# Attention scores in PSUM by halves of the queries: three single banks for scores, four for other products, aims set anew

## The chip, the cores and the metric

The kernel runs on one core of one Trainium2 chip. The metric is the device time of one execution in microseconds (us); lower is better. In the profile, PE is TensorE's matmuls and PEld its weight loads, DVE is VectorE, ACT is ScalarE, POOL is GpSimd and SP is SyncE.

## What is computed

Two graph layers are applied to 16 elements of a batch. An element has 1024 nodes with 256 features (`x`) and an integer adjacency matrix of 1024 by 1024 (`adj`).

The first layer is attention with 8 heads of 32 features, with a leaky slope in place of a scale, and a mask:

```python
q, k, v = heads(features @ Wq), heads(features @ Wk), heads(features @ Wv)
e = einsum('whqd,whkd->whqk', q, k)
e = where(e >= 0, e, 0.2 * e)
attn = softmax(where(adj > 0, e, -9e15), axis=-1)
h = concat_heads(attn @ v)
out = concat([layernorm(h), features]) @ Wffn.T
x1 = layernorm(out) + features
```

The second layer is a graph attention done twice, then a feed-forward block with 1024 hidden values:

```python
Wh = h @ W
e = leaky_relu(Wh @ a[:F] + (Wh @ a[F:]).T, 0.2)
h = softmax(where(adj > 0, e, -9e15), axis=1) @ Wh      # twice: (W1, a1), (W2, a2)
h = layernorm(x1 + h)
out = layernorm(h + relu(h @ w_ff1 + b_ff1) @ w_ff2 + b_ff2)
```

All values are fp32. The kernel uses exponentials without subtracting a maximum (`unshifted_path`); a flag, worked out at its end, would start a general path if the sums or scores left safe limits. In these runs it doesn't.

## The kernel before: stages, order and names

Work is cut into tiles of 128 nodes, 8 tiles (`NT`) an element. The 16 elements `b` are overlapped in a software pipeline: while the scores of element `b` are made, the rest of element `b - 1` (its layer norms, the two graph attentions, the feed-forward block of the element before) and the projections of element `b + 1` (transposes of x, q, k, v, the mask) are fitted between them.

The order of every engine's instructions is written out ahead by a planner, the class `Order`. Each piece of work is a Python generator that yields steps: `on(PE=450)` says that the next instructions occupy an engine for so many ns by the planner's own estimate, `take` and `give` handle a place in a pool of buffers, `wait` and `fire` handle events between pieces. Where several pieces could start within 300 ns (`WINDOW`), the one with the smallest due time (its aim) is put first. An aim is a share of a slot (`SLOT`, 253 us) after the start of the element's scores, from the table `AIM` (`EARLY` for the first two elements). The chip then runs each engine's queue strictly in that order, and each instruction waits for its operands and its buffer; no time of the planner is kept on the chip.

The pieces that matter here:

- `load_stacks` (L536 and on) loads `qs` and `ks`, the operands of one head's scores, by SP's queue (L554). `all_scores` (L567) multiplies them (L587): for a tile `t` of keys it makes a tile `ps_s` of 128 keys by 1024 queries, in two matmuls of 512 columns, one for each PSUM bank. Element 0 takes one such tile at a time, the others two at once, so four matmuls stand in a row. The pool `scores` has two tiles of two banks each.
- `weights` (L594) scales a tile by 0.2 from PSUM into `p` in SBUF (ACT, L605; in element 0 also DVE, L603), takes the maximum of that and the scores on DVE (L607), which frees the tile's two banks, takes the exponential on ACT (L610) and multiplies by the mask on POOL (L614). There are five `p` buffers.
- `all_values` (L617) multiplies `p` of two tiles by v into the one bank `ps_a` (L636; output rows of the two query halves are placed at partitions 0 and 64).
- Every other product goes to the pool `misc`, three single banks `ps_m`: transposes (L355, L417, L663, L807, L915), q and k (L470), v (L499), rows (L739, L742, L771), the two graph products `second_rows` (L862) and `normed_pair` (L887), and the feed-forward block (L927, L955). A bank is freed when ACT or DVE has copied it out (L311 and L313, L475, L506 and L508, L670, L774, L870, L933 and L936 among others).
- `attend` (L824, L827, L830, L832) makes a tile of graph attention on DVE and scales rows on ACT, eight tiles a layer, two layers an element.
- `mask_part`, `x_pair` and `qk_part` issue the loads of `adj` and `x` (ACT's queue) and the stores of q and k halves (SP's queue).

So PSUM's eight banks are: scores 2 x 2, misc 3, values 1. `lead` in `AIM` bounds how far ahead of its due time a score may be put, `fast0`, `fast1` and `fast15` scale the pace of the scores in the first two and the last element.

Of the kernel before, what the change touches and what calls it, by code (L numbers as in the profile page):

```python
# [9 lines left out]
FT = mybir.dt.float32  # L10
# [4 lines left out]
AF = mybir.ActivationFunctionType  # L15
OP = mybir.AluOpType

ALPHA = 0.2
EPS = 1e-5
H = 8  # L20
P = 128
HALF = 512
# [155 lines left out]
def on(shared=False, delay=0.0, **costs):  # L178
    return "on", (costs, shared, delay)
# [6 lines left out]
def wait(event):  # L186
    return "wait", event


def fire(event):  # L190
    return "fire", event


def take(pool):
    return "take", pool


def give(pool):
    return "give", pool


def start(thread, aim):
    return "start", (thread, aim)
# [21 lines left out]
def unshifted_path(  # L225
# [8 lines left out]
    nc = tc.nc  # L234
    B, N, D = x.shape
    NT = N // P
# [5 lines left out]
    NH = N // HALF  # L242
# [4 lines left out]
    YW = D + 2  # L247
    NSUM = NT * H + 2 * NT
    NSCORE = 4 * NT
    SLOT = 253e3  # L250
    PACE = SLOT / (H * NT // 2)


    AIM = dict(mask0=0.759, x=0.818, x_step=0, mask=0.747, mask_step=0.0264, qk0=0.614, qk1=0.898,
               qk_step=0.0231, v0=0.832, v1=0.974, v_step=0.0591, rows=-0.244, rows_step=0.0408, first0=0.12,
               first1=0.252, graph0=-0.009, graph1=0.21, graph_step=0, second=0.355, second_step=0.0335,
               normed=0.78, normed_step=0.026, ff_wait=(None, 0, 1, 0), ff=(0.532, -0.011, 0.487, 0.497),
               ff_step=0.0386, fast0=0.425, fast1=0.938, fast15=0.832, lead=3.15)

    EARLY = dict(x=0.87, x_step=0.005, mask=0.747, mask_step=0.0296, qk0=0.692, qk1=0.909, qk_step=0.0345,  # L260
                 v0=0.774, v1=1.001, v_step=0.0568, rows=-0.139, rows_step=0.0071, first0=0.082, first1=-0.169,
                 graph0=-0.195, graph1=-0.027, graph_step=0, second=0.302, second_step=0.0335, normed=0.781,
                 normed_step=0.02, ff_wait=(None, 0, 1, 0), ff=(0.633, -0.001, 0.488, 0.497), ff_step=0.0386)
# [3 lines left out]
    small = ctx.enter_context(tc.tile_pool(name="small", bufs=6))  # L267
    psum = ctx.enter_context(tc.tile_pool(name="psum", bufs=2, space=bass.MemoryType.PSUM))
    dram = ctx.enter_context(tc.tile_pool(name="dram", bufs=3, space=bass.MemoryType.DRAM))
    bufs = dict(misc=3, scores=2, acc=1, p=5, stacks=2, stage=2, adj=2, adjb=2, pair=18,  # L270
                xT=2, v=2, mask=2, hn=1, w8=2, big=1, job=1)
    work = Order(**bufs)

# [111 lines left out]
    stacks = {}  # L385
# [41 lines left out]
    def make_mask(b, t0):  # L427
# [3 lines left out]
        for n, (t, halves) in enumerate(parts):  # L431
            yield start(mask_part(b, t, halves),
                        t0 + ((share(b - 1, "mask") if b else AIM["mask0"]) + share(b - 1, "mask_step") * n) * SLOT)

# [123 lines left out]
    probs = {}  # L558
# [8 lines left out]
    def all_scores():  # L567
        for b in range(B):
            yield wait(("stack", b, 0))
            t0 = begin[b] = work.now  # L570
            if b + 1 < B:
                yield start(project(b + 1, t0), t0)
            for h in range(H):
                yield wait(("stack", b, h))
                q, kk = stacks[b, h]
                n = 2 if b else 1
                for t in range(0, NT, n):
                    due = t0 + (h * NT + t) / 2 * pace(b)
                    yield aim(due, AIM["lead"] * PACE)
                    for _ in range(n):  # L580
                        yield take("scores")
                    ps = [psum.tile([P, N], FT, tag="scores", name="ps_s") for _ in range(n)]
                    yield on(PE=450 * n)
                    for i in range(n):
                        for nh in range(NH):
                            cols = slice(nh * HALF, (nh + 1) * HALF)
                            nc.tensor.matmul(ps[i][:, cols], kk[:, (t + i) * P:(t + i + 1) * P], q[:, cols],  # L587
                                             start=True, stop=True)
                    if t + n == NT:
                        yield give("stacks")  # L590
                    for i in range(n):
                        yield start(weights(b, h, t + i, ps[i]), due + i * PACE / 2)

    def weights(b, h, t, ps):  # L594
        yield take("p")
        p = buf([P, N], "p", "p")
        probs[b, h, t] = p
        if b == 0:
            engine = yield on(ACT=1050, DVE=1230)
        else:  # L600
            engine = yield on(ACT=1050)
        if engine == "DVE":
            nc.vector.tensor_scalar(p, ps, ALPHA, None, op0=OP.mult)  # L603
        else:
            nc.scalar.activation(p, ps, AF.Copy, scale=ALPHA)  # L605
        yield on(DVE=1220)
        nc.vector.tensor_tensor(p, p, ps, op=OP.max)  # L607
        yield give("scores")
        yield on(ACT=1080)
        nc.scalar.activation(p, p, AF.Exp)  # L610
        for tt in range(NT):
            yield wait(("mask", b, tt, t // TPH))
        yield on(POOL=2050, shared=True)
        nc.gpsimd.tensor_tensor(p, p, mask_of(b, t), op=OP.mult)  # L614
        yield fire(("p", b, h, t))
# [815 lines left out]
```

## Time and profile before

| | |
|---|---|
| median of 3 runs | 4489.06 us (4487.12 to 4491.18) |
| profiled execution | 4494.55 us, span 4492.7 us |
| mean granted TensorE clock | 0.99 |
| busy: PE, DVE, ACT, POOL | 4326.9, 3315.8, 2886.4, 2472.5 us |
| scores: ACT L605, DVE L607, 128x1024 | mean 1025 and 1214 ns, 993 and 1024 times |
| exponential L610, mask product L614 | mean 1058 and 2195 ns, 1024 times each |
| score matmul L587, start to start in a row | about 233 ns, 2048 times |

The page of a profile gives busy time by engine, then the span in 40 slices (tenths busy), then the queues of DMAs, a chain of work followed back from the end, and groups of instructions by line. The other views used here answer from the same trace: busy time in stretches of the span that one chooses, waits (an engine's idle time, put down to the instruction that ended it), and a timeline of single instructions, in which neighbours of one kind are merged (x2, x8). An fp32 matmul of the program stands twice in the trace, that of the scores once. A busy PE is not PE at its peak, since matmuls overlap.

### The profile page before, as it was taken

The numbers are of one execution on the slowest core, as the hardware profiler recorded it, in microseconds if no ns is written. First come the engines' busy times: TensorE is split into PE (matmuls) and PEld (weight loads), VectorE is DVE, ScalarE is ACT, GpSimd is POOL, SyncE is SP. The second block draws the span as 40 slices with busy tenths as digits, with TensorE's granted clock in tenths as the row PEclk, the third lists the DMA queues.
The fourth block names the chain that finished last, engine by engine and source line by source line (L and its number), as shares of the span: only waits on it lengthen the run. The fifth ranks groups of instructions, "written<-read, shape, count | busy, mean of one in ns | idle before, by whom it ended". The sixth has DMA issues, their size and how long they took to land.

```text
span 4492.7 us, 57101 instructions
## 1 busy us (share of the span) xinstructions
PE 4326.9 (96%) x20299; PEld 2871.2 (64%) x20299; DVE 3315.8 (74%) x5262; ACT 2886.4 (64%) x4015; POOL 2472.5 (55%) x1544
## 2 busy tenths in 40 slices
PE   7888999999999999999999999999999999999998
PEld 3444656667666666766667666676666667666587
DVE  6877767787776877778777776877778777776754
ACT  5666575666666666666666666666666666666631
POOL 5756565564565556556554565546556554665610
PEclk9989999999999999999999999999999999999999
DMA  6422223232232322223231232322223231231100
GB/s 188 113 66 83 70 59 90 61 99 61 75 97 60 106 59 80 81 63 99 64 103 53 73 98 65 101 64 80 79 65 99 64 101 54 71 94 53 26 22 20
DMA packets 156208, 343.57 MB, mean 76 GB/s; under 512 B 21750, under 2 KB 24332, under 8 KB 155916
## 3 DMA queue, kind: packets, MB, share of 16 engines
q1 hardware_dynamic: 109836, 255.93, 20.1%
q10 hardware_dynamic: 46080, 83.91, 6.3%
q8 instruction: 164, 2.69, 0.2%
q14 instruction: 128, 1.05, 0.1%
HBM read 239.09 MB, written 100.66 MB: 76 GB/s over the span
## 4 chain that ended last, share of the span: by engine, by line
PE 68%; DVE 17%; POOL 5%; issue 5%; ACT 2%; POOLq 0%; ACTq 0%; DVEq 0%
PE ps_a L636 15%; PE ps_s L587 9%; PE ps_m L887 8%; PE ps_m L862 8%; PE ps_m L927 7%; PE ps_m L955 6%; DVE att L827 5%; DVE att L824 5%; POOL p L614 4%; DVE p L607 3%; PE ps_m L771 3%; PE ps_m L739 2%; PE ps_m L742 2%; PE ps_m L355 2%; PE ps_m L470 2%
## 5 line engine op out<-in xcount | busy, mean ns | idle before, releaser
L614 POOL TENSOR_TENSOR p<-p,mask 128x1024 f32<-128x1024 f32 x1024 | 2230.1, 2195 | 1570.6 <-ACT p L610 1460.2
L607 DVE TENSOR_TENSOR p<-p,ps_s 128x1024 f32<-128x1024 f32 x1024 | 1211.2, 1214 | 403.9 <-ACT p L605 402.4
L610 ACT ACTIVATE p<-p 128x1024 f32<-128x1024 f32 x1024 | 1081.1, 1058 | 377.5 <-DVE p L607 355.2
L605 ACT ACTIVATE p<-ps_s 128x1024 f32<-128x1024 f32 x993 | 973.0, 1025 | 188.4 <-PE ps_s L587 169.7
L636 PE MATMUL ps_a<-p,v 128*33 128x512 f32 (+1 forms) x4096 | 999.3, 606 | 28.9 <-POOL p L614 27.3
L587 PE MATMUL ps_s<-qs,ks 128*128 128x512 f32 x2048 | 635.0, 428 | 37.4 <-DVE p L607 34.7
L587 PEld LDWEIGHTS ps_s<-qs,ks 128*128 128x128 f32 x2048 | 349.9, 190 | 341.0 <-DVE p L607 97.2
L636 PEld LDWEIGHTS ps_a<-p,v 128*33 128x33 f32 (+1 forms) x4096 | 199.6, 114 | 534.5 <-issue 401.1
L887 PE MATMUL ps_m<-y,att 128*128 128x256 f32 x2048 | 480.6, 381 | 12.7 <-ACT v L508 11.0
L955 PE MATMUL ps_m<-wf,hid 128*128 128x256 f32 x2048 | 478.3, 383 | 10.6 <-ACT xT L313 8.9
L927 PE MATMUL ps_m<-rT,wf 128*128 128x256 f32 x2048 | 477.3, 382 | 9.0 <-ACT z L313 3.5
L862 PE MATMUL ps_m<-y,att 128*128 128x258 f32 x2048 | 472.7, 381 | 0.0
L955 PEld LDWEIGHTS ps_m<-wf,hid 128*128 128x128 f32 x2048 | 381.8, 191 | 79.1 <-issue 14.8
L862 PEld LDWEIGHTS ps_m<-y,att 128*128 128x128 f32 x2048 | 385.9, 190 | 63.9 <-issue 3.6
L887 PEld LDWEIGHTS ps_m<-y,att 128*128 128x128 f32 x2048 | 375.4, 189 | 77.1 <-ACT v L508 13.1
L927 PEld LDWEIGHTS ps_m<-rT,wf 128*128 128x128 f32 x2048 | 379.4, 191 | 60.3 <-ACT z L313 3.8
L824 DVE SCALAR_TENSOR_TENSOR att<-first,second 128x1024 f32<-128x1024 f32 x256 | 354.1, 1383 | 73.2 <-ACT first L811 73.2
L827 DVE SCALAR_TENSOR_TENSOR att<-mask,att 128x1024 f32<-128x1024 fp8e4 x256 | 357.8, 1398 | 8.7
L832 ACT ACTIVATE y<-y,check 128x258 f32<-128x258 f32 x256 | 130.9, 511 | 312.4 <-DVE check L830 292.9
L338 POOL TENSOR_SCALAR rs<-mv 128x2 f32<-128x2 f32 (+1 forms) x224 | 57.6, 257 | 421.6 <-DVE mv L335 421.5
L407 DVE TENSOR_SCALAR adj_b<-adj_i 128x512 fp8e4<-128x512 int32 x256 | 229.8, 940 | 22.0 <-DMA adj_i<-in_adj_dram 12.2
L936 ACT ACTIVATE hid<-ps_m,columns 128x256 f32<-128x256 f32 x372 | 158.9, 471 | 117.2 <-PE ps_m L927 91.6
(103 smaller groups left out, 4243.7 us busy)
## 6 DMA issues: line engine op xcount, KB each, us to landing
adj_i<-in_adj_dram ACTq DMA_DIRECT2D x256, 256.0 KB, 3.4
qs<-qk_halves SPq DMA_DIRECT2D x256, 256.0 KB, 4.2
ks<-qk_halves SPq DMA_DIRECT2D x256, 256.0 KB, 5.0
qk_halves<-high SPq DMA_DIRECT2D x128, 256.0 KB, 3.6
qk_halves<-low SPq DMA_DIRECT2D x128, 256.0 KB, 5.2
xr<-in_x_dram ACTq DMA_DIRECT2D x64, 256.0 KB, 3.0
x_kept<-x SPq DMA_DIRECT2D x64, 256.0 KB, 2.3
x<-x_kept SPq DMA_DIRECT2D x64, 256.0 KB, 5.1
```

The lines of the kernel that those rows point to most:

```text
L587: nc.tensor.matmul(ps[i][:, cols], kk[:, (t + i) * P:(t + i + 1) * P], q[:, cols], start=True, stop=True)
L605: nc.scalar.activation(p, ps, AF.Copy, scale=ALPHA)
L607: nc.vector.tensor_tensor(p, p, ps, op=OP.max)
L610: nc.scalar.activation(p, p, AF.Exp)
L614: nc.gpsimd.tensor_tensor(p, p, mask_of(b, t), op=OP.mult)
L636: nc.tensor.matmul(acc[nh * 64:nh * 64 + m, :], v[:, t, c:c + m], p[:, nh * HALF:(nh + 1) * HALF], start=(t == 0), stop=(t == NT - 1))
L824: nc.vector.scalar_tensor_tensor(e, first[:, 0, :], second[:, j:j + 1], first[:, 1, :], op0=OP.mult, op1=OP.max)
L827: nc.vector.scalar_tensor_tensor(e, mask_of(b, j), -1.0, e, op0=OP.mult, op1=OP.mult, accum_out=sums[:, j:j + 1])
L862: nc.tensor.matmul(pa[:, cols:cols + width], big[:, j, i * P:(i + 1) * P], rows[:, j, :width], start=(j == 0), stop=(j == NT - 1))
L887: nc.tensor.matmul(pa[:, i * D:(i + 1) * D], big[:, j, t * P:(t + 1) * P], y2[:, j, :D], start=(j == 0), stop=False)
L927: nc.tensor.matmul(pa[:, i * 2 * P:(i + 1) * 2 * P], wf1[:, dc, hc * P:(hc + 1) * P], rT[:, dc, :], start=(dc == 0), stop=(dc == DC - 1))
L955: nc.tensor.matmul(pa[:, i * D:(i + 1) * D], hid[hc // 2][:, hc % 2, i * P:(i + 1) * P], wf2[:, hc, :], start=(hc == 0), stop=False)
```

## The change

A tile of scores is no longer one object of two banks. `all_scores` takes one bank at a time and issues one matmul of 512 queries, then starts a piece `leaky` for that half, which scales it into its half of `p` (ACT; in element 0 also DVE) and takes the maximum on DVE, and frees the one bank. `weights` takes the `p` buffer, waits for both halves, and goes on as before with the whole tile (exponential, mask). The pool `scores` has three single banks and `misc` four; values keep one. The numbers in `AIM` are new, those in `EARLY` are not.

```diff
-    AIM = dict(mask0=0.759, x=0.818, x_step=0, mask=0.747, mask_step=0.0264, qk0=0.614, qk1=0.898,
-               qk_step=0.0231, v0=0.832, v1=0.974, v_step=0.0591, rows=-0.244, rows_step=0.0408, first0=0.12,
-               first1=0.252, graph0=-0.009, graph1=0.21, graph_step=0, second=0.355, second_step=0.0335,
-               normed=0.78, normed_step=0.026, ff_wait=(None, 0, 1, 0), ff=(0.532, -0.011, 0.487, 0.497),
-               ff_step=0.0386, fast0=0.425, fast1=0.938, fast15=0.832, lead=3.15)
+    AIM = dict(mask0=0.692, x=0.693, x_step=0.0077, mask=0.726, mask_step=0.017, qk0=0.792, qk1=0.947,
+               qk_step=0.0271, v0=0.861, v1=1.013, v_step=0.0734, rows=-0.098, rows_step=0.0408,
+               first0=0.028, first1=0.191, graph0=0.001, graph1=0.204, graph_step=0, second=0.355,
+               second_step=0.0084, normed=0.78, normed_step=0.026, ff_wait=(None, 0, 1, 0),
+               ff=(0.483, -0.011, 0.466, 0.497), ff_step=0.0386, fast0=0.429, fast1=0.946,
+               fast15=0.464, lead=3.42)
...
-    bufs = dict(misc=3, scores=2, acc=1, p=5, stacks=2, stage=2, adj=2, adjb=2, pair=18,
+    bufs = dict(misc=4, scores=3, acc=1, p=5, stacks=2, stage=2, adj=2, adjb=2, pair=18,
...
-                n = 2 if b else 1
-                for t in range(0, NT, n):
+                for t in range(NT):
                     due = t0 + (h * NT + t) / 2 * pace(b)
                     yield aim(due, AIM["lead"] * PACE)
-                    for _ in range(n):
+                    yield start(weights(b, h, t), due)
+                    for nh in range(NH):
                         yield take("scores")
-                    ps = [psum.tile([P, N], FT, tag="scores", name="ps_s") for _ in range(n)]
-                    yield on(PE=450 * n)
-                    for i in range(n):
-                        for nh in range(NH):
-                            cols = slice(nh * HALF, (nh + 1) * HALF)
-                            nc.tensor.matmul(ps[i][:, cols], kk[:, (t + i) * P:(t + i + 1) * P], q[:, cols],
-                                             start=True, stop=True)
-                    if t + n == NT:
+                        ps = psum.tile([P, HALF], FT, tag="scores", name="ps_s", bufs=bufs["scores"])
+                        yield on(PE=225)
+                        nc.tensor.matmul(ps, kk[:, t * P:(t + 1) * P], q[:, nh * HALF:(nh + 1) * HALF],
+                                         start=True, stop=True)
+                        yield start(leaky(b, h, t, nh, ps), due)
+                    if t == NT - 1:
                         yield give("stacks")
-                    for i in range(n):
-                        yield start(weights(b, h, t + i, ps[i]), due + i * PACE / 2)
-
-    def weights(b, h, t, ps):
+
+    def leaky(b, h, t, nh, ps):
+        yield wait(("p open", b, h, t))
+        part = probs[b, h, t][:, nh * HALF:(nh + 1) * HALF]
+        if b == 0:
+            engine = yield on(ACT=610, DVE=690)
+        else:
+            engine = yield on(ACT=610)
+        if engine == "DVE":
+            nc.vector.tensor_scalar(part, ps, ALPHA, None, op0=OP.mult)
+        else:
+            nc.scalar.activation(part, ps, AF.Copy, scale=ALPHA)
+        yield on(DVE=690)
+        nc.vector.tensor_tensor(part, part, ps, op=OP.max)
+        yield give("scores")
+        yield fire(("leaky", b, h, t, nh))
+
+    def weights(b, h, t):
         yield take("p")
         p = buf([P, N], "p", "p")
         probs[b, h, t] = p
-        if b == 0:
-            engine = yield on(ACT=1050, DVE=1230)
-        else:
-            engine = yield on(ACT=1050)
-        if engine == "DVE":
-            nc.vector.tensor_scalar(p, ps, ALPHA, None, op0=OP.mult)
-        else:
-            nc.scalar.activation(p, ps, AF.Copy, scale=ALPHA)
-        yield on(DVE=1220)
-        nc.vector.tensor_tensor(p, p, ps, op=OP.max)
-        yield give("scores")
+        yield fire(("p open", b, h, t))
+        for nh in range(NH):
+            yield wait(("leaky", b, h, t, nh))
         yield on(ACT=1080)
         nc.scalar.activation(p, p, AF.Exp)
```

More of the change, by code (lines that the diff above doesn't have):

```diff
@@ L249, in unshifted_path @@
     NSCORE = 4 * NT
-    SLOT = 253e3
+    SLOT = 253000.0
     PACE = SLOT / (H * NT // 2)
-    AIM = dict(mask0=0.759, x=0.818, x_step=0, mask=0.747, mask_step=0.0264, qk0=0.614, qk1=0.898,
-               qk_step=0.0231, v0=0.832, v1=0.974, v_step=0.0591, rows=-0.244, rows_step=0.0408, first0=0.12,
-               first1=0.252, graph0=-0.009, graph1=0.21, graph_step=0, second=0.355, second_step=0.0335,
-               normed=0.78, normed_step=0.026, ff_wait=(None, 0, 1, 0), ff=(0.532, -0.011, 0.487, 0.497),
-               ff_step=0.0386, fast0=0.425, fast1=0.938, fast15=0.832, lead=3.15)
+    AIM = dict(mask0=0.692, x=0.693, x_step=0.0077, mask=0.726, mask_step=0.017, qk0=0.792, qk1=0.947,
[4 more added lines that the diff above has]
+               fast15=0.464, lead=3.42)
     EARLY = dict(x=0.87, x_step=0.005, mask=0.747, mask_step=0.0296, qk0=0.692, qk1=0.909, qk_step=0.0345,
```

## The prediction, made before the changed kernel was run

> **What bounds the kernel now.** I read the page's busy shares and slices first, then busy time by stage, then what TensorE (PE) waited for, then single instructions in the timeline.
>
> ```profile
> PE 4326.9 (96%) x20299; PEld 2871.2 (64%) x20299; DVE 3315.8 (74%) x5262; ACT 2886.4 (64%) x4015; POOL 2472.5 (55%) x1544
> PE   7888999999999999999999999999999999999998
> PEclk9989999999999999999999999999999999999999
> ```
>
> PE is the engine without slack; only the first 700 us and the last 400 show holes. I cut the span where the scores of an element begin (first score matmuls of elements 0, 1, 2, 3, 4 and 15, and the last score of all): us, then busy PE, PEld, DVE, ACT, POOL, then the granted clock.
>
> ```profile
> 45.00:205.00 160.00, 134.83 (x559) 55.56 (x560) 142.95 (x142) 113.72 (x135) 134.95 (x65) 0.95 0.49 138
> 205.00:481.00 276.00, 242.84 (x1053) 144.50 (x1051) 197.93 (x289) 171.11 (x226) 163.34 (x89) 0.91 0.25 72
> 1034.00:4006.00 2972.00, 2929.93 (x13908) 1957.44 (x13904) 2241.97 (x3575) 2005.37 (x2783) 1677.39 (x1057) 1.00 0.28 78
> 4006.00:4264.00 258.00, 242.94 (x1117) 162.24 (x1116) 190.42 (x284) 165.44 (x222) 152.51 (x90) 0.99 0.14 38
> 4264.00:4493.00 229.00, 215.26 (x1049) 183.45 (x1047) 115.03 (x290) 59.13 (x126) 26.13 (x45) 0.98 0.06 21
> ```
>
> Element 0 (160 us) is paced by VectorE (DVE) and GpSimd (POOL) together. Elements 4 to 14 take 2972/11 = 270.2 us each, and PE is idle for only 42 of 2972 us: there nothing but PE's own waits can be won. What it waited for over the whole span (us, times, longest):
>
> ```profile
> PE ps_s L587 <- DVE p L607: 34.7, 31, 4.1
> PE ps_a L636 <- POOL p L614: 27.3, 33, 2.1
> PE ps_m L887 <- ACT v L508: 11.0, 11, 1.0
> ...
> PE ps_m L955 <- ACT xT L313: 8.9, 12, 0.9
> ...
> PE ps_m L499 <- ACT v L508: 7.3, 12, 1.3
> ```
>
> Line 887 multiplies attention by rows; it has no use for v. It waits because line 508 had not yet emptied one of the three `misc` banks: a wait for a bank, not for data, once in each element. Adding the rows of this list whose releaser only empties a bank of another product (11.0, 8.9, 7.3, then 5.1, 3.5, 2.5, 2.3, 2.1, 1.6 and eight of 1.2 or less, 5.9 together) gives 50 us. The first row, 34.7, is the wait for score banks; by stage it is 11.7 (element 0), 8.4, 2.5 and, in element 15, 12.1. The rest, p from POOL and ho from ACT, is a wait for data. One place where two bank waits follow each other:
>
> ```profile
> 2835.38 1.16 PE L499 MATMUL ps_m<-wv,xT 128*128 128x128 f32 x8 [0.53 <-ACT v L508]
> ...
> 2837.13 0.36 ACT L508 ACTIVATE v<-ps_m 128x256 f32<-128x256 f32 x1
> 2837.54 1.59 PEld L887 LDWEIGHTS ps_m<-y,att 128*128 128x128 f32 x8 [1.19 <-ACT v L508]
> 2837.55 1.99 PE L887 MATMUL ps_m<-y,att 128*128 128x256 f32 x8 [1.00 <-ACT v L508]
> ```
>
> [...] The trace has 1214 (L607) and 679 (L475, a 512-column tensor_tensor out of PSUM). [...] Here 0.95, 0.91 and 0.98 are granted in the first three stages (0.98 in 481 to 762), which is at most 8 + 25 + 6 = 39 us of lost clock.
>
> **The change part by part.** The sum is made against the profiled execution, 4494.55 us (span 4492.7 and 1.85 around it). It lies 5.5 above the median of the runs, 4489.06; I carry the difference over to the median.
>
> *Four misc banks.* A product has to be emptied before the fourth next one and no longer before the third. All 50 us gone is one end; the other is 0, if what stands behind is then late for its data (L955 needs hid, L663 needs ho). The waits last 0.5 to 1.3 us, and a fourth bank gives one more product's time: two L499 groups of four are 1.05 us of PE, eight L887 entries 1.7. That covers most of them. I take two thirds: -33.
>
> *Scores by halves in three banks.* The matmuls are the same 2048 of 512 columns. Before, from element 1 on, a pair of tiles takes both double banks at once: about 0.93 us of PE (4 x 233 ns from start to start), ACT 1.03, DVE 1.21, DVE 1.12 more, so a next pair at best after some 4.5 us, 2.2 a tile. A half holds a bank for 0.23 + 0.58 + 0.68 and two handovers of about 0.1, 1.7 us; three banks give a half every 0.57 us, and DVE at 2 x 0.58 becomes the limit, 1.2 a tile. But less is in flight: one and a half tiles, not two. Ends: all 34.7 gone; or as much again, +20, where a bank is freed behind a long DVE instruction. I take somewhat under half: -15, from elements 0, 1 and 15.
>
> *Twice as many small instructions.* Row durations say 2 x 679 - 1214 = 144 ns more DVE a tile, and on ACT 2 x 587 (512-column copy, L313) - 1025 = 149. Over 1024 tiles that is 147 us of DVE. But neighbours overlap:
>
> ```profile
> 1119.09 1.26 DVE L475 TENSOR_TENSOR low<-ps_m,high 128x512 f32<-128x512 f32 x2
> ```
>
> The second begins 575 ns after the first; two 1024-column maxima begin 1137 apart, so the real price is 2 x 575 - 1137 = 13 ns a tile. Likewise on ACT: 477 between L809 and L811, 920 between two L605, 34 a tile. In elements 3 to 14 either price lies beside PE (DVE works some 204 of 270 us). On the path are the tiles of elements 0, 1, 2 and 15, 256 of them: 256 x 0.013 = 3 us to 256 x 0.147 = 38. I take +3. The new order gives 46 half scalings (23 tiles' worth) to DVE where 31 tiles were; ACT, which takes the rest, had 114 of 160 us in element 0. Nothing taken. One wait is new: the exponential waits for the maxima of both halves, and behind it on ACT stand the next scalings and the emptying of banks. The second maximum comes 0.45 + 0.1 + 0.48 + 0.58 + 0.1 + 0.68 = 2.4 us after the tile's first matmul, where the whole one came after 0.45 + 0.1 + 1.03 + 0.1 + 1.21 = 2.9; so that queue stands no longer.
>
> *More changes of work on PE.* The order has 1023 runs of score matmuls in place of 521, and 511 runs of value matmuls in both. By the starts of single matmuls in the trace, entering scores from another product costs 0 to 0.05 us over streaming; from values 0.195, but going from values to transposes costs 0.15 and to wide products 0.196 as well. Values to scores come 380 times in place of 279: counted with these prices over the whole order, PE's work grows by 4.4 us. Taken +4 (0 to 20).
>
> *Aims.* No instruction is added; every element still holds 260 us of PE work by that count, and after the last score some 210 against 212. x is loaded and transposed 0.125 slots (32 us) earlier: its loads stand in ACT's queue and hold `pair` buffers longer. The q/k projection of the first group moves 0.18 slots later, with its stores and stack loads in SP's queue. Its last part is now due at 0.873 slots, 32 us before the next element; a landing takes 4 to 5 us, so this costs nothing; if that margin were gone, each us late would be a us an element. For the second attention the order leaves 57 us of PE work between the last second_rows product and the first normed one, where there were 32, and for the first 43 in place of 34. DVE needs about 21 us for eight attends. That protects against the added DVE time and is why I charge no more for it. Taken 0 (±15).
>
> Sum: -33 - 15 + 3 + 4 + 0 = -41: profiled 4453.5, on the median 4448. What is late next is p from POOL (27.3 us of waits, left alone) and ho.
>
> **Rivals.** *More comes back.* If all bank waits go (-50), 25 of the score waits, and a third of the lost clock (-13), the sum with +4 is -84: 4405. For it: the idle of elements 0 and 1 [...]. Against: these two are bound by POOL's 137 us and by the attends, neither of which gets shorter.
>
> *Nothing changes.* PE passes the bank and stands at the data one product later: 4489. Against it: at 2837 the attends of the first four tiles, which that product begins with, had ended some 10 us before (one comes every 2.65 us, the last at 2836.3).
>
> *Slower.* Three half banks fall empty in the second attention. Before, its eight attends ran without a score between them. The new order puts one to three half maxima between most of them, and PE's queue is in order: a half that finds no bank holds up the products behind it, and so POOL and ACT after them. An attend is 1.26 + 1.22 + 0.16 = 2.6 us; a half that comes at random behind one waits 1.3. With four such waits of 1.0 us in an element, 13 elements lose 52; with -33 and +4 that is +23: 4512. It decides from (33 - 4)/13 = 2.2 us an element. Against it: the planner's order leaves the 57 us above. For it: in element 15, where scores and attends already mix, the score waits are 12.1 us.
>
> That the change doesn't do what it says is excluded: the built order shows the halves and the new places.
>
> **How the numbers follow.** Forecast (4425 to 4475) 0.44; more comes back 0.22; nothing 0.12; slower 0.22. Faster by over 0.2% (9 us, about what a measurement of this kernel can tell from no change) is 0.66, within it 0.12, slower 0.22. The likeliest gives 4448. The range runs from 4400, leaving out the lower third of the second case, to 4510, leaving out about half of the last: some 0.18.
>
> **What would show it.** In the profile after: rows such as L887 <- v and L955 <- xT gone from PE's waits, an element of about 267 us in place of 270.2, and 4264 to the end unchanged at about 229 us. PE's waits for score banks under 25 us confirm the second step; over 50, in the attends, the slower rival. DVE near 3460 us busy by rows without PE idling more would confirm that overlap hides the small instructions. I am wrong if elements 4 to 14 take 270 or more, or if elements 0 to 2 grow by over 10 us.

## The result and the profile after

The changed kernel takes 4715.6 us (median of 4 runs, 4711.91 to 4720.15) where the kernel before took 4490.12 in the same comparison: a ratio of 1.0498, 95% interval 1.0486 to 1.0511. It is 5% slower. The prediction, 4448 us and faster, was wrong. The profiled execution took 4714.87 us (span 4713.1), 220.3 more than the profiled one before, and the numbers below come from those two.

The page of the changed kernel, busy time and PE's slices:

```profile
PE 4404.3 (93%) x20299; PEld 2891.4 (61%) x20299; DVE 3523.9 (75%) x6437; ACT 2895.4 (61%) x4888; POOL 2497.0 (53%) x1544
PE   7888999999999998999989999899999989998998
```

The holes in PE's row are no longer only at the two ends: six of the last 25 slices show an 8, where before only the very last did. Cut where the scores of elements 0, 1, 4, 15 and the end begin (columns as in the prediction):

```profile
47.00:213.00 166.00, 138.76 (x549) 56.65 (x549) 140.27 (x223) 120.47 (x177) 131.23 (x64) 0.95 0.44 125
...
1050.00:4228.00 3178.00, 3002.91 (x13901) 1977.00 (x13901) 2435.89 (x4392) 1994.46 (x3371) 1726.98 (x1057) 0.99 0.26 74
4228.00:4489.00 261.00, 243.29 (x1114) 160.10 (x1113) 196.09 (x354) 171.42 (x289) 152.18 (x92) 0.99 0.16 41
4489.00:4713.00 224.00, 211.96 (x1036) 181.18 (x1035) 115.93 (x292) 54.12 (x118) 26.83 (x42) 0.99 0.06 21
```

Elements 0 to 2 took 717 us before (160, 276, 281) and take 717 now (166, 269, 282). Element 3 takes 286 (272), element 15 takes 261 (258), the end 224 (229). Elements 4 to 14 take 3178 in place of 2972: 206 of the 220 us are lost in the steady part, where I had expected a small gain. An element there takes 288.9 us in the mean, 287 from element 6 on, in place of 270.2.

Of those 206 us, PE's idle time is 133 (3178 - 3003 = 175, where it was 42). The other 73 are in its busy time. The trace's record of the granted clock had no stretch at half speed between elements 4 and 14 before, and has 23 now (22 of 3.4 us and one of 6.8), 82 us at half speed, with PE busy in 81 of them. In such stretches of this profile a matmul of L867 begins 429 ns after its neighbour, elsewhere 217 (medians), so by my estimate half of the 81, some 41 us, is lost to the clock. What the remaining 32 are made of I have not separated.

What PE waited for over the whole span (us, times, longest):

```profile
PE ps_s L585 <- DVE p L603: 232.7, 167, 12.7
PE ps_m L668 <- ACT ho L314: 14.8, 17, 1.0
...
PE ps_a L641 <- POOL p L619: 4.7, 7, 1.2
```

The rows L887 <- v, L955 <- xT and L499 <- v are gone, as foretold. The wait for p from POOL is down from 27.3 to 4.7. One row has grown from 34.7 to 232.7: score matmuls that wait until a maximum on DVE has freed their bank. In one element (2795 to 3082) it is 13.5 us in 9 waits, and the only other wait there is 1.0 us.

Why the maxima come late is told by the groups of DVE (busy us, mean ns of one; the last columns are idle time before):

```profile
L603 DVE TENSOR_TENSOR p<-p,ps_s 128x512 f32<-128x512 f32 x2048 | 1315.5, 680 | 428.0 <-ACT p L601 421.7
L832 DVE SCALAR_TENSOR_TENSOR att<-mask,att 128x1024 f32<-128x1024 fp8e4 x256 | 484.0, 1890 | 8.8
```

The same instruction of an attend in the kernel before:

```profile
L827 DVE SCALAR_TENSOR_TENSOR att<-mask,att 128x1024 f32<-128x1024 fp8e4 x256 | 357.8, 1398 | 8.7
```

A half maximum lasts 680 ns, as predicted. But the second instruction of an attend lasts 1890 ns in the mean where it was 1398, both times 256 of them. A place in a second attention, while the scores of element 10 are made:

```profile
2968.47 5.21 POOL L619 TENSOR_TENSOR p<-p,mask 128x1024 f32<-128x1024 f32 x2 [3.11 <-ACT p L615]
...
2971.73 3.03 DVE L832 SCALAR_TENSOR_TENSOR att<-mask,att 128x1024 f32<-128x1024 fp8e4 x1
...
2974.88 1.86 DVE L603 TENSOR_TENSOR p<-p,ps_s 128x512 f32<-128x512 f32 x3
...
2975.61 0.50 PE L585 MATMUL ps_s<-qs,ks 128*128 128x512 f32 x1 [2.63 <-DVE p L603]
```

GpSimd multiplies two tiles by the mask from 2968.5 to 2973.7. The attend that begins at 2971.7 ends at 2974.8, about 1.1 us after the mask product, nearly the 1.22 us that it takes alone. Three half maxima stand behind it on DVE, and when the first of them has freed a bank, at 2975.6, PE has stood for 2.63 us. In a second attention of the kernel before, GpSimd had nothing to do while the eight attends ran:

```profile
2811.31 4.24 POOL L614 TENSOR_TENSOR p<-p,mask 128x1024 f32<-128x1024 f32 x2 [1.77 <-ACT p L610]
2838.96 4.24 POOL L614 TENSOR_TENSOR p<-p,mask 128x1024 f32<-128x1024 f32 x2 [23.42 <-ACT p L610]
```

That is GpSimd's whole timeline from 2810 to 2842: 23.4 us without a mask product, from 2815.6 to 2839.0. The eight attends ran on DVE from 2814.1 to 2836.5.

So it is throughout the trace. In the changed kernel 94 attends (L832) begin while a mask product runs: each lasts 3.03 to 3.20 us and ends 1.08 to 1.09 us after that product. The other 162 last 1.22 to 1.23 us, 14 of them beside a mask product that began after them. In the kernel before (L827) only 24 last 3.03 to 3.20. A maximum is not held: 1075 of the 2048 run beside a mask product, and none of the 2048 lasts over 0.69 us (mean 680 ns). An attend has both inputs in SBUF, a maximum one (the other is in PSUM).

Attends are not the only instructions held. Call a DVE instruction held when it lasts over 30% and over 0.2 us longer than a short one of its kind, and take PE's waits for score banks one by one. In 95 of the 232.7 us, the longest hold during the wait or in the 4 us before it is that of an attend (L832 or L829). In 88 us it is that of another instruction: the last layer norm (L971 33, L973 17), rows being normalized (L350 21), the conversion of the mask (L408 17). In 49 us nothing was held. Over the whole trace, holds add up to 474 us of DVE, and they added up to 409 before: the attends' share grew from 72 to 212 us, that of all others fell from 337 to 262. So the kernel before was held nearly as long; what differs is what is held, and how often a score maximum stands behind it.

### The profile page after: what moved, and what is told of

It is laid out like the page before. It is cut to its first block, busy times and chain, and to the rows that moved or that the text cites. A ratio compares the mean times of both kernels' runs of the same rounds, so it can differ in the third digit from the quotient of the medians.

```text
span 4713.1 us, 58895 instructions
## 1 busy us (share of the span) xinstructions
PE 4404.3 (93%) x20299; PEld 2891.4 (61%) x20299; DVE 3523.9 (75%) x6437; ACT 2895.4 (61%) x4888; POOL 2497.0 (53%) x1544
## 4 chain that ended last, share of the span: by engine, by line
PE 59%; DVE 34%; ACT 2%; POOL 2%; issue 1%; DMA 1%; ACTq 0%; SPq 0%; POOLq 0%; DVEq 0%
PE ps_a L641 14%; DVE att L832 10%; PE ps_s L585 8%; PE ps_m L867 8%; DVE att L829 7%; DVE p L603 7%; PE ps_m L892 7%; PE ps_m L932 4%; PE ps_m L960 4%; PE ps_m L776 2%; DVE z L973 2%; PE ps_m L747 2%; PE ps_m L744 2%; PE ps_m L471 2%; PE ps_m L356 2%
## 5 line engine op out<-in xcount | busy, mean ns | idle before, releaser
L619 POOL TENSOR_TENSOR p<-p,mask 128x1024 f32<-128x1024 f32 x1024 | 2262.4, 2218 | 1656.8 <-ACT p L615 1213.6
L603 DVE TENSOR_TENSOR p<-p,ps_s 128x512 f32<-128x512 f32 x2048 | 1315.5, 680 | 428.0 <-ACT p L601 421.7
L601 ACT ACTIVATE p<-ps_s 128x512 f32<-128x512 f32 x2002 | 1092.1, 596 | 332.4 <-PE ps_s L585 320.9
L585 PE MATMUL ps_s<-qs,ks 128*128 128x512 f32 x2048 | 815.2, 470 | 243.7 <-DVE p L603 232.7
L867 PE MATMUL ps_m<-y,att 128*128 128x258 f32 x2048 | 493.6, 388 | 0.0
L892 PE MATMUL ps_m<-y,att 128*128 128x256 f32 x2048 | 490.1, 384 | 0.8 <-ACT y L837 0.8
L832 DVE SCALAR_TENSOR_TENSOR att<-mask,att 128x1024 f32<-128x1024 fp8e4 x256 | 484.0, 1890 | 8.8
L867 PEld LDWEIGHTS ps_m<-y,att 128*128 128x128 f32 x2048 | 393.0, 193 | 73.6 <-issue 9.2
L892 PEld LDWEIGHTS ps_m<-y,att 128*128 128x128 f32 x2048 | 383.2, 192 | 54.3 <-ACT y L837 1.2
L837 ACT ACTIVATE y<-y,check 128x258 f32<-128x258 f32 x256 | 130.8, 511 | 428.8 <-DVE check L835 425.8
L829 DVE SCALAR_TENSOR_TENSOR att<-first,second 128x1024 f32<-128x1024 f32 x256 | 369.5, 1443 | 28.7 <-ACT first L816 25.2
L350 DVE TENSOR_SCALAR y<-y,mv,rs 128x256 f32<-128x256 f32 x256 | 158.9, 658 | 68.8 <-POOL rs L341 68.8
L341 POOL TENSOR_TENSOR rs<-rs,minus_half 128x2 f32<-128x2 f32 (+1 forms) x224 | 174.8, 780 | 17.2
```

The lines of the kernel that those rows point to most:

```text
L585: nc.tensor.matmul(ps, kk[:, t * P:(t + 1) * P], q[:, nh * HALF:(nh + 1) * HALF], start=True, stop=True)
L601: nc.scalar.activation(part, ps, AF.Copy, scale=ALPHA)
L603: nc.vector.tensor_tensor(part, part, ps, op=OP.max)
L829: nc.vector.scalar_tensor_tensor(e, first[:, 0, :], second[:, j:j + 1], first[:, 1, :], op0=OP.mult, op1=OP.max)
L832: nc.vector.scalar_tensor_tensor(e, mask_of(b, j), -1.0, e, op0=OP.mult, op1=OP.mult, accum_out=sums[:, j:j + 1])
L867: nc.tensor.matmul(pa[:, cols:cols + width], big[:, j, i * P:(i + 1) * P], rows[:, j, :width], start=(j == 0), stop=(j == NT - 1))
```

## The experiments

The theory after the result: in the new order mask products stand between the attends, the two hold each other up, the maxima queue behind the attends that are held, and PE's queue, which is in order (the 20299 matmuls of the profile follow each other, line by line, as in the built program), stands at a half score. The rivals: the new aims alone do it; three banks are too few; the planner thinks of a bank as free too exactly, so that any delay is felt. Where an expectation uses letters, H says that the halves and not the aims do the harm, P that mask products hold the attends and so make the maxima late, S that twice as many small instructions cost that much, and Q that it is the missing slack in the plan.

**The two parts one by one.** The changed kernel with the old `AIM` (e1_old_aims), and the kernel before with the new one (e2_new_aims):

```diff
-    AIM = dict(mask0=0.692, x=0.693, x_step=0.0077, mask=0.726, mask_step=0.017, qk0=0.792, qk1=0.947,
...
+    AIM = dict(mask0=0.759, x=0.818, x_step=0, mask=0.747, mask_step=0.0264, qk0=0.614, qk1=0.898,
...
```

> The changed kernel (halves, 3 score banks, 4 misc banks) with the aims of the kernel before. Theory H (the halves: score maxima now stand between the attends of a graph attention, a score half waits for its bank behind an attend [...], and TensorE's queue stands still): in this order too, seven gaps between attends of one attention an element hold 2 to 3 maxima, so it stays slow, 4640 to 4720 us, and TensorE waits over 150 us for score maxima. Rival A (the new aims alone did it): near the kernel before or better, 4440 to 4510 us. Rival S (twice as many small instructions, whatever their order): as the changed kernel, 4700 to 4730.

> The kernel before (whole tiles of scores, 3 misc banks) with the new aims. Theory H: the attends stand together as before in most elements, so it is within 1.5% of the kernel before, 4480 to 4550 us, with under 60 us of waits for score maxima. Rival A (aims): 4650 to 4720 us. Rival S: as the kernel before, 4490.

Measured: 4693.43 us (ratio 1.0450, 1.0433 to 1.0468) and 4807.2 (1.0701, 1.0683 to 1.0718). Halves, single issue and banks with the old aims cost 203 us, with 180.6 us of waits for score banks, as expected. The aims alone cost 316, both together 225. The parts don't add up, and the second expectation fell: the aims are not harmless. Their harm on whole tiles is another one, as PE's waits show:

```profile
PE ps_m L888 <- ACT y L833: 111.5, 7, 18.7
PE ps_s L588 <- DVE p L608: 82.6, 69, 5.0
PE ps_m L888 <- DVE hn L671: 70.3, 6, 17.3
```

I read the two rows of L888, 13 waits of up to 18.7 us, as normed products put ahead of attends that are not yet done: an attention placed too late. In the changed kernel L892, the same line, waits 0.8 us. So the new aims belong to the new order, and what halves, single issue and banks lose together is the first run's.

**More score banks, and the grain of issue.** Four half banks and three of `misc` (e3_four_halves); four halves taken at once, as the pairs were, with the old aims (e6_halves_in_fours); the kernel before with one whole tile at a time (e7_whole_single):

```diff
-    bufs = dict(misc=4, scores=3, acc=1, p=5, stacks=2, stage=2, adj=2, adjb=2, pair=18,
+    bufs = dict(misc=3, scores=4, acc=1, p=5, stacks=2, stage=2, adj=2, adjb=2, pair=18,
```

```diff
-                for t in range(NT):
+                n = 2 if b else 1
+                for t in range(0, NT, n):
...
-                    for nh in range(NH):
+                    for _ in range(n * NH):
                         yield take("scores")
```

```diff
-                n = 2 if b else 1
+                n = 1
```

> The changed kernel with four single score banks and three misc banks, aims of the changed kernel. Theory H says that what is short is score banks while VectorE is away: with one more, the waits for score maxima fall by a third or more and the time to 4560 to 4650 us, and the waits for misc banks (L892 behind v and the like) come back, some 40 us. If the bank count doesn't matter but maxima between attends do (they stand there in this order too, in both attentions), it stays at 4680 to 4730. Rival S: 4700.

> Halves, but issued as before: two tiles at a time from element 1 on, four halves taken together in four single banks, three misc banks, old aims. Each half still has its own scaling and maximum and frees its own bank. No maximum stands between attends in this order. Theory P: near the kernel before, 4470 to 4560 us. If small instructions cost (rival S): 4600 or more. If any order but the one that the aims were made for is slow: 4600 to 4750, with waits that have nothing to do with scores.

> The kernel before, in which every element (not only element 0) issues whole tiles of scores one at a time. Maxima stand between attends in some of the elements (8 and 11 of those looked at, 1 or 2 in a gap). Theory P: between, 4540 to 4640 us, most of it in elements of that kind. If halves are what hurts: 4480 to 4520. If single issue hurts by itself: 4640 to 4720.

Measured: 4931.64 us (1.0977, 1.0959 to 1.0996), 4725.87 (1.0516, 1.0497 to 1.0535) and 4827.93 (1.0751, 1.0733 to 1.0768). None came out as theories H and P had it: e3 and e7 are slower than any case foresaw, and e6 lies where its third case has it, that any order but the one that the aims were made for is slow. A fourth score bank, taken from `misc`, makes it worse: waits for score banks 264.3 us, an attend 2116 ns. So one more score bank is no cure. And halves are not needed for the loss. With whole tiles and the old aims, a change of one number gives the same picture, score waits of 190.5 us and

```profile
L827 DVE SCALAR_TENSOR_TENSOR att<-mask,att 128x1024 f32<-128x1024 fp8e4 x256 | 536.3, 2095 | 8.8
```

against 1398 before. Nor do pairs keep the attends from being held, once they are of halves (L837, the same attend, 1766 ns in e6). But PE waits only 74.1 us for score banks in e6, which loses 234: most of its loss is another one, spread over many rows, and I have not separated it.

**Keeping the attends together.** In its plan the planner serializes the steps of DVE and GpSimd that are marked `shared`, and a rule (L155) says who goes first when an attend and a mask product are both possible. e5_attends_together widens the preference for DVE:

```diff
-                lead = 100.0 if engine == "DVE" else -100.0
+                lead = 400.0 if engine == "DVE" else -400.0
```

> The changed kernel with one rule of the planner altered: [...] VectorE now goes first if it can start within 400 ns (100 before), so that in the order no score maximum stands between the attends of elements 5, 8 and 11, and no mask product between attends either. Theory P ([...] VectorE, held there, is late with the score maxima; TensorE stands at a score half): L832 falls from 1890 to under 1500 ns on average, the waits for score maxima from 233 to under 100 us, the time to 4470 to 4580 us. Rival (the score queue itself is too short, with or without attends): 4650 to 4720 us with over 180 us of such waits.

Measured: 4694.43 us (1.0448, 1.0430 to 1.0465). The step that I wanted was done, the attend is at 1296 ns, and still only 21 us came back: the expectation fell. The waits for score banks are

```profile
PE ps_s L585 <- DVE p L603: 162.4, 127, 12.7
```

Taken one by one as above, none of these has an attend as its longest hold. In 112 us it is one of the four other instructions (L971 47, L350 34, L408 23, L973 8), and in 51 nothing was held, about as much as in the changed kernel. So held attends are not the cause by themselves: when they are out of the way, other held instructions stand ahead of the maxima. For this order that is read from the trace alone; no run here shortens its mask product.

**Slack in the plan.** The planner is told that a half is ready 1.5 or 3 us later than it computes (e9_slack_1500, e10_slack_3000, and e11_slack_old_aims with the old aims), so that it would leave the bank more time:

```diff
         nc.vector.tensor_tensor(part, part, ps, op=OP.max)
+        yield pause(1500)
         yield give("scores")
```

> The changed kernel in which the planner believes that a score bank comes free 1.5 us after its maximum. Nothing is slower on the chip; only the order changes: a score half is put later in TensorE's queue, behind more other products. Theory Q (the order has no slack between a maximum and the next half in its bank, so every delay of VectorE that the planner does not foresee becomes a wait of TensorE): score waits fall from 233 to under 120 us, the time to 4540 to 4640 us. Rival (VectorE has too much work in these stretches, whatever the order): 4680 to 4760 us.

> As the run before with 3 us in place of 1.5. Theory Q: 4480 to 4600 us, score waits under 60 us, unless the scores then run so late that TensorE waits for the weights from GpSimd instead (L641 behind L619 over 50 us). Rival: 4680 to 4800 us.

> Halves with 1.5 us of slack and the aims of the kernel before. Theory Q: better than the same without slack (4693), 4520 to 4630 us. If the aims matter more than the slack: as the run with slack and the new aims only within 1%.

Measured: 4844.17 us (1.0786, 1.0768 to 1.0804), 5061.34 (1.1269, 1.1250 to 1.1287), 4818.87 (1.0728, 1.0710 to 1.0746). The waits for score banks halve (109.7, 118.6, 89.0 us), but with 3 us p from POOL makes PE wait 131.3 us, and many smaller rows grow. All three expectations fell, and this theory is dropped: each plan with more slack was slower than the same plan without, and the attends are still at 1792 to 1839 ns.

**A shorter mask product.** This shortens what the attends wait for, and leaves the order and the PSUM bank of every tile as they were. If the loss hangs on the length of the mask product, it shrinks with it, and the changed kernel comes close to the kernel before; if not, e4 stays over 4680 us. GpSimd multiplies 512 or 128 of 1024 columns: the changed kernel (e4_half_mask, e13_after_eighth), the kernel before (e8_before_half_mask, e14_before_eighth), and the two mixed ones (e15_old_aims_eighth is e1, e16_new_aims_eighth is e2):

```diff
-        nc.gpsimd.tensor_tensor(p, p, mask_of(b, t), op=OP.mult)
+        nc.gpsimd.tensor_tensor(p[:, :HALF], p[:, :HALF], mask_of(b, t)[:, :HALF], op=OP.mult)
```

> The changed kernel in its own order of instructions, in which GpSimd multiplies only the first 512 columns of a tile of weights by the mask; the other half stays unmasked. [...] If [...] that is what the score banks wait for, L832 falls to about 1.4 us, TensorE's waits for score maxima from 233 to under 120 us, and the time to 4530 to 4600 us. [...]

> Control for the half mask: the kernel before, in its own order, with GpSimd multiplying only the first 512 columns by the mask, the other half unmasked. Read from the trace, to the end of the last output row of the fast path (4487.2 us in the kernel before; the general path may follow). Theory P: [...] it gains under 80 us, against 248 in the changed kernel, and the two end within 1.5% of each other. If a shorter mask product simply speeds either kernel alike: it gains some 200 us too.

> The changed kernel in its own order, GpSimd multiplying 128 of 1024 columns by the mask (the rest stays unmasked). Read to the end of the last output row of the fast path. [...] 4360 to 4410 us, within 1% of the kernel before with the same cut. If halves and their order cost by themselves: 4430 to 4480.

> The kernel before in its own order with the same cut of the mask product to an eighth: from 4393 with the half to 4340 to 4380 us, [...].

> Halves with the old aims (4693 us) and the mask product cut to an eighth. [...] 4360 to 4430 us; if the halves lose in another way: over 4500.

> Whole tiles with the new aims (4807 us) and the mask product cut to an eighth. Its waits were for whole attentions (L888 behind L833 and hn) that the order puts too late, [...] 4500 to 4650 us. [...]

In these the general path follows (17,691 to 17,958 us in all), so what is read is the end of the last output row of the first path, from one profile each:

| columns of the mask product | its length, us | changed, us | before, us | difference |
|---|---|---|---|---|
| whole | 2.2 | 4707.6 | 4487.2 | +220.4 |
| half | 1.2 | 4459.4 | 4392.7 | +66.7 |
| eighth | 0.47 | 4374.7 | 4367.4 | +7.3 |

The waits for score banks in the changed kernel, with half of the mask product and with an eighth:

```profile
PE ps_s L585 <- DVE p L603: 88.8, 105, 12.8
```

```profile
PE ps_s L585 <- DVE p L603: 44.9, 34, 12.8
```

They were 232.7 us with the whole of it. The attend goes from 1890 to 1497 to 1263 ns, and all holds on DVE add up to 4.5 us with an eighth. 213 of the 220 us hang on how long GpSimd's mask product lasts. e4 ends some 70 us earlier than I had expected, and the kernel before gains 94.5 us with half a mask product where I had expected under 80; the eighths came out within their ranges. With an eighth, an element takes 265.2 us in the changed kernel, from element 6 on, and 266.8 in the one before (by stages, the changed one gains 9.8 us in elements 4 to 14 and 5.0 at the end, and loses 16.5 in elements 0 to 3, 2.6 in element 15 and 2.8 at the start). The mixed ones: e15 ends at 4427.3 (4685.0 with the whole mask), so 138 of the 198 us that e1 loses to the kernel before go the same way; e16 at 4610.8 (4803.3), so most of e2's loss is not this. Its two rows of late attentions are still there, with 92.8 and 88.8 us.

**Another attend.** The second instruction of an attend with one input in SBUF, as a maximum has; the mask of the graph attention is left out with it. On the changed order (e12_attend_no_port) and on the order before (e17_before_attend_no_port):

```diff
-        nc.vector.scalar_tensor_tensor(e, mask_of(b, j), -1.0, e, op0=OP.mult, op1=OP.mult,
-                                       accum_out=sums[:, j:j + 1])
+        nc.vector.tensor_scalar(e, e, 1.0, None, op0=OP.mult, op1=OP.add,
+                                accum_out=sums[:, j:j + 1])
```

> The changed kernel in its own order, in which the second operation of an attend (L832) multiplies by 1.0 and sums, with one SBUF input in place of two: the graph attention's mask is left out. [...] it falls to about 1.3 us; with it go its share of the score waits (55 us of L832 itself, and part of the maxima behind it), so the waits fall from 233 to 130 to 180 us and the time to 4600 to 4660 us. If the attends are only where the waits show and the maxima are late anyway: over 4690 us.

> [...] the kernel before, in its own order, with the second operation of an attend (L827) multiplying by 1.0 and summing, one SBUF input in place of two, so the graph attention's mask is left out. There L827 is 1398 ns on average, most attends running while GpSimd is idle: if it is the overlap with mask products that costs, the gain is under 40 us (4450 to 4490), against 128 in the changed kernel. If the edit is simply a faster attend: 100 us or more.

Measured, one run each: 4587.14 us, 128 fewer than the changed kernel, and 4582.17, 94 more than the kernel before, where I had expected no more than before. Both attends last 1220 ns. The second looked like a blow to the theory, but its new waits are these:

```profile
PE ps_m L499 <- DVE low L475: 62.7, 11, 5.9
PE ps_m L955 <- DVE low L475: 54.6, 11, 5.0
```

Line 499 has no use for `low`; it wants its bank. In the built program of e17 the order of every engine is that of the kernel before, but of the 4032 stretches in which PE fills one PSUM tile 1301 lie in another bank (1116 of 5196 in e12). Banks are given when the program is built, and the new instruction changed that. With the mask cut to an eighth none differs. So these two runs measure two things at once, and I don't count them for the theory or against it.

**GpSimd as busy, but reading nothing.** The cut mask also gave GpSimd time and p earlier. f1_mask_written is the changed kernel in which GpSimd writes a constant over p twice in place of the product. If what it reads in SBUF is what holds the attends, they return to 1.22 us; if it is the time that it works, they don't. Order and banks are those of the changed kernel:

```diff
-        nc.gpsimd.tensor_tensor(p, p, mask_of(b, t), op=OP.mult)
+        for _ in range(2):
+            nc.gpsimd.memset(p, 1.0)
```

> The changed kernel, but GpSimd no longer multiplies p by the mask: it writes the constant 1.0 twice over the 1024 columns of p, which should take about as long (from the 0.30 us of a constant written over 248 columns, some 1.1 us each, 2.2 together) and reads nothing. The attention of the first layer is thereby left out (every weight is 1). The order of every engine and the bank of every PSUM tile are those of the changed kernel. [...] attends return to under 1300 ns in the mean (1890), waits for score banks to under 100 us (232.7), and the first path ends at 4380 to 4480 us (4707.6 in the changed kernel, 4487.2 in the one before). Rival: what counts is how long GpSimd works on a tile, and when p is ready, not what it reads: attends near 1890 ns or waits for score banks above 180 us, an end of 4650 or later. If writing alone holds the attends as well, the numbers are the rival's and the two are told apart by the mean of the attend: [...].

The general path follows here too. The first path ends at 4410.9 us, 297 before the changed kernel's. The two writes take 2 x 0.96 = 1.9 us of GpSimd (2.2 for the product). The attend, and PE's waits for score banks up to 4420 us:

```profile
L833 DVE SCALAR_TENSOR_TENSOR att<-mask,att x256: 1224/1225/1227, 271.2 to 4317.1; 128x1024 f32<-128x1024 fp8e4 x128
```

```profile
PE ps_s L585 <- DVE p L603: 59.4, 49, 12.7
```

The three durations are the shortest, the middle and the longest of 256: not one attend was held. An element takes 266.6 us from element 6 on, and elements 4 to 14, where 206 of the 220 us were lost, take 2939: the kernel before takes 2935 there, both with half of the mask product and with an eighth. So in the steady part it is the mask product, which reads SBUF, and not the time that GpSimd works, that costs the changed kernel nearly all that it loses. For the whole span this is not measured, since the kernel before was not run with the writes; f1's end lies 18 and 44 us behind its ends with half and with an eighth.

Two instructions with only one input in SBUF are still held in f1: L350, up to 1245 ns where its shortest takes 394, and L408, up to 1679 (407); some 20 of the 59.4 us stand behind them. So two inputs in SBUF are not what every held instruction has, and no run here tells what holds these.

No version here that computes the whole result is faster than the kernel before.

## Why the prediction was wrong, step by step

*What bounds the kernel* was right: PE, and its own waits. *Four misc banks, -33*: right in kind. The three rows named are gone, and no other took their place. Its size shows only where the mask product is down to 0.47 us (e13 against e14): 1.6 us per steady element and 10 over elements 4 to 14, and that is what is left of banks, halves and changes of work together, for which I had -33 - 15 + 4.

*Scores by halves, -15*: this is the step that failed. The waits for score banks went from 34.7 to 232.7 us, not to 20, and an estimated 41 us lost to the half clock came with them. My upper end was +20, "where a bank is freed behind a long DVE instruction"; I had the place and not the length. I reckoned a bank's turn from a chain of ACT and DVE durations in which DVE was free when ACT was done. It was not: GpSimd's mask products held the attends and other instructions that stood ahead of the maxima (474 us of holds, 4.5 with an eighth of the product), and with GpSimd only writing (f1) the waits are 59.4 us.

*Small instructions, +3*: in the steady elements nothing speaks against it; in e13 an element with twice as many small instructions is shorter than one without. On the path, in elements 0 to 2 and 15, the changed kernel takes 18 us more than the one before (e13 against e14): within the 3 to 38 of the prediction, but not its 3, and I can't tell small instructions from the rest there. DVE's busy time grew by 208 us, not 147; by rows the maxima grew by 104 and the attend L832 by 126 (some others fell), and the second part is not work but time in which it stood. *"In elements 3 to 14 either price lies beside PE (DVE works some 204 of 270 us)"* is the sentence that misled: a share of busy time doesn't tell how late a short instruction is in a queue that is in order and in which instructions ahead of it can be held.

*Changes of work, +4*: can't be told apart; it lies within the 265.2 us. *Aims, 0 (±15)*: with halves the new aims cost 22 us (4715.6 - 4693.4), a little outside; with whole tiles 316. The 57 us of PE work that protect the second attention did what I said, L892 waits 0.8 us. But what I protected was the attends' consumer; what suffered was the maxima in the attends' queue.

*The slower rival* had the place and the chain of waits: half banks empty in the second attention, maxima between attends. It lacked what makes the attends long, and so was mis-sized in two terms. I priced an attend at 2.6 us, from a stretch where GpSimd was idle; with a mask product beside it 4.45 us pass (1.26 + 3.03 + 0.16). And I took four waits of 1.0 us an element; it is nine of 1.5, 13.5 us, and the slower clock on top. Its own point of decision was 2.2 us an element. About half of the waits with a hold stand behind instructions that the rival does not name.

Could it have been seen? The trace before had the sign, though not in the rows that I read. All instances of the attend in the kernel before, shortest, middle and longest:

```profile
L827 DVE SCALAR_TENSOR_TENSOR att<-mask,att x256: 1224/1225/3204, 265.4 to 4393.4; 128x1024 f32<-128x1024 fp8e4 x128
```

An instruction of fixed size that lasts 1225 ns or 3204 is being held by something: the 24 long ones all begin while a mask product runs. Its mean of 1398 was 44 us above 256 x 1.225, and L968 had 1102 ns in the mean where its shortest takes 453. The next question would have been what GpSimd does during the attends, and whether the new order still leaves it nothing to do: the 23.4 us gap was there to be seen, and the new order, singly issued, gave no reason to think that it would stay. With whole tiles issued singly (e7) it is lost: in an attention whose eight attends run from 2907.9 to 2956.3, GpSimd's longest pause is 6.8 us.

A half maximum is as short as I had reckoned (680 ns, where the whole took 1214). What the halves also did here was to let other work in between.

## What to carry to other kernels

Before an order is made finer, list the instructions on VectorE and GpSimd that hold each other up (here an attend, 1.22 us alone and 3.03 behind a mask product) and look at what runs beside each now: a quiet partner (23.4 us without a mask product around eight attends) may be what makes the present order good. The sum of held time is not the measure (409 us before, 474 after); what stands behind each hold is. An engine with a quarter of its time free (DVE, 75% busy) can still set the end, if short instructions that free buffers stand in its queue behind long ones that can be held. Aims and due times fit one order; halves with old aims (4693.4 us), and old tiles with new aims (4807.2), were both slower than the kernel before (4490.1).

## What the hardware showed that I had not expected

- A held instruction is no gap in the profile: L832 shows as 3.03 us of busy DVE. The spread of its durations (1224 to 3199 ns) gives it away, and f1 removes it (1224 to 1227).
- It works both ways: where attend and mask product of the changed kernel both begin at 2958.94, the attend lasts 1.23 us and the mask product 3.22 in place of 2.12.
- With PE's stalls came 23 stretches of half clock in elements 4 to 14, where there had been none; e13 has two there and f1 one. In the 3.4 us before each of them, as long as a stretch is, PE was busy for 13 to 52% of the time, and no pause of PE in these elements is longer than 3.02 us. In the kernel before, no pause there is longer than 1.0 us.
- Changing one instruction's form moved about a third of the PSUM tiles to other banks with the order unchanged, and on the order before it came with 94 us more.
